# Cross-attention and feed-forward block on one core: adapters accumulated in the base banks, statistics shared between DVE and ACT, written order for PE and DVE, paired transposes

## The chip, the cores and the metric

The kernel runs on one core of one Trainium2 chip. The metric is the device time of one execution in microseconds (us). PE is the matmul engine, DVE the vector engine, ACT the activation engine, POOL the general-purpose engine, SP the engine that issues the loads and stores. The five run side by side and are tied by semaphores; each one runs its own instructions in order.

## The reference

The block takes x of 16 x 64 tokens with 512 features. The first half is a cross-attention with 32 heads of 128 and a bias per head. The second half is a linear layer with a routed low-rank adapter:

```
x = x + xattn(layernorm(x), ctx, mask, bias)         # 32 heads, S = 64
n = layernorm(x)
base   = n @ base_W.T + base_b                       # 512 -> 512
probs  = softmax(n @ router_W.T + router_b)          # 15 routes
w      = sum over the top 8 of probs, mapped by expert_map to 8 experts
h      = n @ A.T                                     # 8 experts x rank 16 = 128
lora   = ((h * w) @ B) * 2
x = x + base + lora
```

All of it is in 32-bit floats. A product is made of three matmuls on halves: each operand is split into a high part (rounded to the matmul's format) and the low rest, and high x high, high x low and low x high are summed.

## The kernel before

Tokens are handled as eight tiles of 128 rows (`NT` = 8). Keys, values and queries are computed in a seven-product scheme over blocks. The heads then run in 16 pairs. For each pair a string `steps` sets what stands after what: `S` is the scores and softmax of two heads, `Q` a step of the queries of the next pair, `O` the output projection of one token tile for the previous pair (`proj_o`, six matmuls of 512 columns, and one DVE add into `acc`), `T` the transpose of one head's probabilities (`transpose_p`, four transposes and one ACT copy). After the string comes `pv_mm`, the product of probabilities and values, with four casts on ACT (`oh`) and four subtracts on DVE (`ol`). PE's order is the written one during attention; the other engines are ordered by a scheduler with priorities, where `tc.high_priority(offset=SOON)` moves an instruction ahead.

The feed-forward stage follows. Its weights lie side by side in `bh` and `bl`, 656 columns each: 128 columns of adapter input A, 15 of the router, one empty column (together `NB` = 144) and then 512 of the base layer. A bank of PSUM holds 512, so each tile takes two groups of matmuls: group A with columns 0 to 255 (L583 to L585 with 128x256; the adapter input, the router and the first 112 base columns), and group B with columns 256 to 655 (the same lines with 128x400). Each group is 12 matmuls. For one tile t the steps are:

- `ffn_norm` (L561): on DVE bn_stats (L88), its aggregate (L89), a small add (L91) and, after POOL's power (L92), a small product (L94); then ACT writes the normalised tile xn (L96).
- `ffn_bias` (L567): POOL adds the base bias to the residual tile, giving xb (L569).
- `ffn_in` (L572): PE transposes xn (L100, four transposes), ACT casts to x2h (L68), DVE subtracts to x2l (L69).
- `ffn_a` (L588): group A; then the routing on DVE, line L592 to L612, with one exponential on ACT (L595), the sum of exponentials (L597), its reciprocal (L599), the scaling of the probabilities (L601), the choice of the top 8 (L603 to L606), the weights by expert (L608, L610) and the weighted adapter input hw (L612). ACT copies the first 112 base columns to o1 (L615).
- `ffn_b` (L618): six matmuls of group B; the transpose of hw (L622); its split into hh (ACT) and hl (DVE); the other six matmuls of B; three adapter matmuls of 512 into a third bank (L634 to L636). For the first six tiles ACT copies B to o1 (L628) and POOL adds xb (L629); for the last two POOL adds 112 columns (L631) and DVE the other 400 (L632). DVE then adds the adapter bank (L637), and SP stores the tile (L638).

The written order of the stage is: six output projections of the last pair, with the norms of tiles 0 to 2 among them; the transposes of tile 0, the seventh projection, the transposes of tile 1, group A of tile 0; then a loop over t in which the norm of t+3, the transposes of t+2, group A of t+1 and `ffn_b` of t follow each other. Only POOL keeps this order strictly (`tc.manual_schedule(engines={nc.gpsimd.engine})`); PE, DVE and ACT are ordered by the scheduler.

Of the kernel before, what the change touches and what calls it, by code (L numbers as in the profile page):

```python
# [25 lines left out]
E = 8  # L26
# [6 lines left out]
OUT_AHEAD = 6  # L33
# [12 lines left out]
def xattn_ffn_kernel(ctx: ExitStack, tc: tile.TileContext, x, ctxT, wq, wk, wv, wo, fside, mask,  # L46
# [58 lines left out]
    with ExitStack() as actx:  # L105
# [208 lines left out]
        with tc.manual_schedule(engines={nc.tensor.engine}):  # L314
# [114 lines left out]
            def pv_mm(i, pt, v):  # L429
                ps = [bank() for _ in range(2)]  # L430
                for u in range(NT):
                    for b in range(2):
                        r = slice(b * S, (b + 1) * S)
                        for d in range(0, P, S):
                            c = slice(i * P + d, i * P + d + S)
                            nc.tensor.matmul(ps[b][d:d + S, u * S:(u + 1) * S], lhsT=v[u // 2][r, u % 2, c],  # L436
                                             rhs=pt[r, u, :], start=True, stop=True)
                res = []
                for b in range(2):
                    hl = [blk("o", f"o{c}", F32R) for c in "hl"]  # L440
                    split(hl[0], hl[1], ps[b])
                    res.append(hl)
                return res
# [60 lines left out]
            for p in range(NP):  # L504
# [5 lines left out]
                steps = "SOOOOOOTOTO" if last else "QSQQOOQOQOOQOQOTOT" if p else "SQQQQQTQQT"  # L510
                pts, t, n = [], 0, 0
                for c in steps:
# [5 lines left out]
                    elif c == "Q":  # L518
                        nxt(1)
                        n += 1  # L520
                        if n == 3:
                            w = load_o(p)
                        if n == 7 and p + 2 < NP:
                            after = Queries(load_pair(p + 2), ORDER)
                        if n == 7 and p + 2 == NP:
                            sar = [blk("raw", "sar", F32, (P, 2, NB)) for _ in range(2)]
                            sbw = [blk("raw", "sbw") for _ in range(KC)]
                            for i in range(2):
                                nc.gpsimd.memset(sar[i][:, :, NAR:NB], 0.0)
                                nc.sync.dma_start(out=sar[i][:, :, 0:NAR], in_=arT[:, 2 * i:2 * i + 2])  # L530
                            for kc in range(KC):
                                nc.sync.dma_start(out=sbw[kc], in_=base_wT[:, kc])
                    elif c == "T":
                        pts.append(transpose_p(ps[len(pts)]))
                    else:
                        proj_o(t, *prev)
                        t += 1
                        if last and t == 2:
                            w = load_o(p)
                qs, nxt = nxt, after  # L540
            prev = ([pv_mm(i, pts[i], v) for i in range(2)], w)
# [6 lines left out]
    slb = blk("g", "slb")  # L548
    nc.sync.dma_start(out=slb, in_=lora_b)
# [8 lines left out]
    lbh = fw.tile([P, D], F32R, name="lbh")  # L558
    lbl = fw.tile([P, D], F32R, name="lbl")
    split(lbh, lbl, slb)  # L560
    def ffn_norm(t):  # L561
        xt = acc[:, t, :]
        xn = fs2.tile([P, D], F32, tag="xn", name="xn2", bufs=3)
        norm(fs2, [xn], [xt])
        return xn
# [6 lines left out]
    def ffn_in(xn):  # L572
# [4 lines left out]
        split(x2h, x2l, ps)  # L577
        return x2h, x2l

    def ffn_mm(o, x2h, x2l, w, kcs=range(KC)):  # L580
        for kc in kcs:
            a = x2h[:, kc * P:(kc + 1) * P]
            nc.tensor.matmul(o, lhsT=a, rhs=bh[:, kc, w], start=kc == 0, stop=False)  # L583
            nc.tensor.matmul(o, lhsT=a, rhs=bl[:, kc, w], start=False, stop=False)
            nc.tensor.matmul(o, lhsT=x2l[:, kc * P:(kc + 1) * P], rhs=bh[:, kc, w],  # L585
                             start=False, stop=kc == KC - 1)

    def ffn_a(x2h, x2l):  # L588
        pa = bank()
        ffn_mm(pa[:, 0:NA], x2h, x2l, slice(0, NA))  # L590
# [4 lines left out]
        nc.scalar.activation(lg, lg, AF.Exp, bias=nm)  # L595
        sme = fs2.tile([P, 1], F32, tag="sme", name="sme2")
        nc.vector.tensor_reduce(sme, lg, AX.X, ALU.add)  # L597
        rc = fs2.tile([P, 1], F32, tag="rc", name="rc2")
        nc.vector.reciprocal(rc, sme)  # L599
        pr = fs2.tile([P, NR], F32, tag="pr", name="pr")  # L600
        nc.vector.tensor_scalar(pr, lg, rc, None, ALU.mult)  # L601
        top = fs2.tile([P, 8], F32, tag="top", name="top")
        nc.vector.max(top, pr)  # L603
        rest = fs2.tile([P, NR], F32, tag="rest", name="rest")
        nc.vector.match_replace(rest, top, pr, 0.0)
        nc.vector.tensor_tensor(pr, pr, rest, ALU.subtract)  # L606
        we = fs2.tile([P, E, NR], F32, tag="we", name="we")
        nc.vector.tensor_tensor(we, oneh, pr.unsqueeze(1).to_broadcast([P, E, NR]), ALU.mult)  # L608
# [3 lines left out]
        nc.vector.tensor_tensor(hw, pa[:, 0:E * R].rearrange("p (e r) -> p e r", e=E),  # L612
                                w8.unsqueeze(2).to_broadcast([P, E, R]), ALU.mult)
        o1 = fs2.tile([P, D], F32, tag="o1", name="o1", bufs=4)
        nc.scalar.copy(o1[:, 0:NA - NB], pa[:, NB:NA])  # L615
        return hw, o1

    def ffn_b(t, xb, x2h, x2l, hw, o1):  # L618
        po = bank()[:, 0:NF - NA]
        ffn_mm(po, x2h, x2l, slice(NA, NF), (0, 1))  # L620
# [4 lines left out]
        split(hh, hl, pt[:, 0:P])  # L625
        ffn_mm(po, x2h, x2l, slice(NA, NF), (2, 3))
        if t < NT - 2:
            nc.scalar.copy(o1[:, NA - NB:D], po)  # L628
            nc.gpsimd.tensor_tensor(o1, o1, xb, ALU.add)  # L629
        else:  # L630
            nc.gpsimd.tensor_tensor(o1[:, 0:NA - NB], o1[:, 0:NA - NB], xb[:, 0:NA - NB], ALU.add)  # L631
            nc.vector.tensor_tensor(o1[:, NA - NB:D], xb[:, NA - NB:D], po, ALU.add)  # L632
        pl = bank()
        nc.tensor.matmul(pl, lhsT=hh, rhs=lbh, start=True, stop=False)  # L634
        nc.tensor.matmul(pl, lhsT=hh, rhs=lbl, start=False, stop=False)
        nc.tensor.matmul(pl, lhsT=hl, rhs=lbh, start=False, stop=True)  # L636
        nc.vector.tensor_tensor(o1, o1, pl, ALU.add)  # L637
        nc.sync.dma_start(out=out[t], in_=o1)  # L638

    def out_proj(a, b):  # L640
        for t in range(a, b):
            proj_o(t, *prev)

    xns, xbs, x2s, hws = [], [], [], []
    with tc.manual_schedule(engines={nc.gpsimd.engine}):
        for t in range(OUT_AHEAD):
            out_proj(t, t + 1)
            if t < 3:
                xns.append(ffn_norm(t))
        xbs.append(ffn_bias(0))  # L650
        x2s.append(ffn_in(xns[0]))
        out_proj(OUT_AHEAD, OUT_AHEAD + 1)
        xbs.append(ffn_bias(1))
        x2s.append(ffn_in(xns[1]))
        hws.append(ffn_a(*x2s[0]))
        for t in range(NT):
            if t + OUT_AHEAD + 1 < NT:
                out_proj(t + OUT_AHEAD + 1, t + OUT_AHEAD + 2)
            if t + 3 < NT:
                xns.append(ffn_norm(t + 3))  # L660
            if t + 2 < NT:
                xbs.append(ffn_bias(t + 2))
                x2s.append(ffn_in(xns[t + 2]))
            if t + 1 < NT:
                hws.append(ffn_a(*x2s[t + 1]))
            ffn_b(t, xbs[t], *x2s[t], *hws[t])
# [42 lines left out]
```

## Time and profile before

| what | value |
|---|---|
| median of three runs | 793.68 us (793.59 to 794.07) |
| profiled execution, time | 795.94 us |
| profiled execution, span of the core | 794.2 us |
| granted PE clock | 1.00 |
| PE busy | 778.5 us of the span |
| DVE busy | 589.1 us |
| ACT busy | 413.0 us |
| POOL busy | 144.0 us |
| feed-forward stage (742 to 794 us) | PE 44.99, DVE 43.06, ACT 18.05, POOL 21.95 us busy |

The span is the time of the core's own instructions; the execution's time has what lies around them too. A busy time of PE has overlaps in it: matmuls are pipelined, and one 512-column matmul of this kernel takes 0.39 us but the next one starts 0.23 us later. So PE's cost is read from start to start.

### The profile page before, as it was taken

The numbers are of one execution on the slowest core, as the hardware profiler recorded it, in microseconds if no ns is written. First come the engines' busy times: TensorE is split into PE (matmuls) and PEld (weight loads), VectorE is DVE, ScalarE is ACT, GpSimd is POOL, SyncE is SP. The second block draws the span as 40 slices with busy tenths as digits, with TensorE's granted clock in tenths as the row PEclk, the third lists the DMA queues.
The fourth block names the chain that finished last, engine by engine and source line by source line (L and its number), as shares of the span: only waits on it lengthen the run. The fifth ranks groups of instructions, "written<-read, shape, count | busy, mean of one in ns | idle before, by whom it ended". The sixth has DMA issues, their size and how long they took to land.

```text
span 794.2 us, 18002 instructions
## 1 busy us (share of the span) xinstructions
PE 778.5 (98%) x6944; PEld 673.7 (85%) x6944; DVE 589.1 (74%) x1056; ACT 413.0 (52%) x1154; POOL 144.0 (18%) x146
## 2 busy tenths in 40 slices
PE   7999999999999999999999999999999999999997
PEld 6988999999999999978888888888888888888786
DVE  6997656555557555678878787878777887878986
ACT  6655444454444444674664566455655466456342
POOL 1011000000006002033311332033202230210352
PEclk9999999999999999999999999999999999999999
DMA  7675545454545543375553364335553455241011
GB/s 269 207 244 200 173 159 186 160 186 160 185 160 171 174 159 133 127 237 170 173 170 90 129 186 161 107 124 171 161 157 97 147 175 171 84 148 56 1 42 66
DMA packets 66374, 120.56 MB, mean 152 GB/s; under 512 B 7536, under 2 KB 8176, under 8 KB 66288
## 3 DMA queue, kind: packets, MB, share of 16 engines
q1 hardware_dynamic: 66288, 119.42, 45.8%
q8 instruction: 54, 0.88, 0.5%
q14 instruction: 32, 0.26, 0.1%
HBM read 83.74 MB, written 35.65 MB: 150 GB/s over the span
## 4 chain that ended last, share of the span: by engine, by line
PE 88%; DVE 7%; ACT 2%; DMA 2%; issue 1%; POOL 0%; SPq 0%; ACTq 0%; DVEq 0%; POOLq 0%
PE ps L222 77%; PE pss L404 4%; PE ps L436 4%; PE pst L423 2%; PE yzv L222 1%; ACT p L412 1%; DMA cT<-in_ctxT 1%; DVE o L637 1%; DVE pr L606 1%; DVE x2l L69 1%; DVE nb L94 1%; DVE gl L69 0%; PE pst L100 0%; DVE we L608 0%; DMA so<-in_wo 0%
## 5 line engine op out<-in xcount | busy, mean ns | idle before, releaser
L68 ACT CAST gh<-s 128x512 fp32r<-128x512 f32 (+1 forms) x128 | 65.6, 514 | 147.3 <-PE ps L222 139.3
L69 DVE TENSOR_TENSOR gl<-s,gh 128x512 fp32r<-128x512 f32 (+1 forms) x128 | 73.3, 572 | 44.5 <-ACT gh L68 44.4
L452 DVE TENSOR_TENSOR acc<-acc,ps 128x512 f32<-128x512 f32 x128 | 86.1, 681 | 21.6 <-PE ps L222 20.7
L412 ACT ACTIVATE p<-p,nm 128x64 f32<-128x64 f32 x256 | 85.5, 336 | 31.6 <-DVE nm L409 31.6
L222 PE MATMUL ps<-wh,oh 128*128 128x512 f32 x256 | 101.4, 397 | 0.0
L222 PE MATMUL ps<-wl,oh 128*128 128x512 f32 x256 | 99.9, 391 | 0.0
L222 PE MATMUL ps<-wh,ol 128*128 128x512 f32 x256 | 99.7, 390 | 0.0
L157 POOL TENSOR_TENSOR s<-rq 128x256 f32<-128x256 f32 x32 | 25.2, 788 | 290.4 <-DMA rq<-in_wq 206.5
L395 POOL TENSOR_TENSOR bm<-bm,maskb 128x512 f32<-128x512 f32 x32 | 50.0, 1582 | 73.1 <-DVE maskb L342 40.8
L69 DVE TENSOR_TENSOR gl<-raw,gh 128x512 fp32r<-128x512 f32 x48 | 34.1, 712 | 31.4 <-ACT gh L68 31.4
L222 PEld LDWEIGHTS ps<-wl,oh 128*128 128x128 f32 x256 | 48.1, 188 | 10.1
L222 PEld LDWEIGHTS ps<-wh,ol 128*128 128x128 f32 x256 | 48.1, 188 | 9.9 <-DVE ol L69 0.5
L222 PEld LDWEIGHTS ps<-wh,oh 128*128 128x128 f32 x256 | 48.1, 188 | 9.5
L68 ACT CAST gh<-raw 128x512 fp32r<-128x512 f32 x48 | 29.7, 621 | 47.8 <-PE ps L222 36.6
L69 DVE TENSOR_TENSOR ol<-ps,oh 128x512 fp32r<-128x512 f32 x64 | 39.8, 683 | 15.6 <-ACT oh L68 15.6
L412 ACT ACTIVATION_READ_ACCUMULATOR p<-p,nm 128x1 f32 x256 | 48.1, 188 | 0.0
L69 DVE TENSOR_TENSOR gl<-rq,gh 128x256 fp32r<-128x256 f32 x48 | 32.9, 687 | 11.4 <-ACT gh L68 11.4
L479 DVE TENSOR_TENSOR q<-u,ps 128x512 f32<-128x512 f32 x48 | 32.6, 680 | 10.6 <-PE ps L222 10.6
L68 ACT CAST oh<-ps 128x512 fp32r<-128x512 f32 x64 | 33.1, 590 | 7.7 <-PE ps L436 7.7
L92 POOL TENSOR_TENSOR rs<-rs,nhalf 128x1 f32<-128x1 f32 x16 | 9.5, 595 | 152.1 <-DVE rs L91 109.2
L404 PEld LDWEIGHTS pss<-kT,q 128*64 128x64 f32 x1024 | 31.2, 138 | 5.6 <-PE ps L222 5.0
L436 PEld LDWEIGHTS ps<-pt,v 64*64 64x64 f32 x2048 | 31.4, 135 | 3.3 <-ACT gh L68 2.2
(226 smaller groups left out, 2273.7 us busy)
## 6 DMA issues: line engine op xcount, KB each, us to landing
kd<-c SPq DMA_DIRECT2D x64, 256.0 KB, 2.6
vd<-c SPq DMA_DIRECT2D x64, 256.0 KB, 2.8
v<-vd SPq DMA_DIRECT2D x64, 256.0 KB, 4.3
kT<-kd SPq DMA_DIRECT2D x64, 256.0 KB, 5.4
raw<-in_wk SPq DMA_DIRECT2D x32, 256.0 KB, 3.0
raw<-in_wv SPq DMA_DIRECT2D x32, 256.0 KB, 3.0
bm<-in_fside SPq DMA_DIRECT2D x32, 256.0 KB, 5.7
rq<-in_wq SPq DMA_DIRECT2D x32, 256.0 KB, 5.5
```

What stands on the lines that cost most here:

```text
L68: nc.scalar.copy(hi, src)
L69: (lo_eng or nc.vector).tensor_tensor(lo, src, hi.bitcast(F32), ALU.subtract)
L92: nc.gpsimd.tensor_tensor(rs, rs, nhalf[:, 0:n], ALU.pow)
L157: self.eng.tensor_tensor(r, a, b, op)
L222: nc.tensor.matmul(o, lhsT=a, rhs=b, start=first and n == 0, stop=last and n == 2, skip_group_check=True)
L395: nc.gpsimd.tensor_tensor(bm, bm, maskb, ALU.add)
L404: nc.tensor.matmul(ps[a * S:(a + 1) * S, t, :], lhsT=qT[n // 8][:, c], rhs=kT[n // 8][:, c], start=True, stop=True)
L412: nc.scalar.activation(p[:, t, :], p[:, t, :], AF.Exp, bias=nm[:, t:t + 1], accum_out=sme[:, t:t + 1])
L423: nc.tensor.transpose(ps[:, g * P:(g + 1) * P], p[:, 2 * g:2 * g + 2, :].rearrange("p t k -> p (t k)"), ident)
L436: nc.tensor.matmul(ps[b][d:d + S, u * S:(u + 1) * S], lhsT=v[u // 2][r, u % 2, c], rhs=pt[r, u, :], start=True, stop=True)
L452: nc.vector.tensor_tensor(acc[:, t, :], acc[:, t, :], ps, ALU.add)
L479: nc.vector.tensor_tensor(self.blocks[key], s[u], b[bk], ALU.add)
```

## The change

Five things are done at once.

1. The adapter's product goes into the two banks that already hold the base layer. The weights `lbh` and `lbl` are widened from 512 to 656 columns with zeros in the first 144, and a tile's three adapter matmuls of 512 into a third bank become three of 400 into B's bank and three of 256 into A's bank. ACT's two copies to o1 and POOL's add go away. DVE adds xb to 400 columns from B's bank and to 112 from A's bank. The last tile's two parts are stored apart, one from SP and one from ACT.
2. The statistics of tiles 0 to 2 stay on DVE, now with priority. Those of tiles 3 to 7 go to ACT: one pass that sums, one that sums the squares of the differences, with small steps on ACT and POOL between them.
3. In the routing, the exponential's own accumulator gives the sum, and the reciprocal is applied in the last product instead of in a step of its own.
4. The order of the feed-forward stage is written: PE and POOL from its start, DVE too from the loop on. Five output projections stand ahead of tile 0's transposes instead of six, and nine matmuls of B stand behind the transpose of hw instead of six. The previous pair's eighth output projection is moved behind the last pair's `pv_mm`, whose results go to another pool. The load of the adapter's weights is issued during the last pair but one.
5. In the 14 middle pairs the two transposes `T` stand next to each other: `...OQOTOT` becomes `...OQOTTO`.

```diff
-            def pv_mm(i, pt, v):
+            def pv_mm(i, pt, v, home="o"):
...
-                steps = "SOOOOOOTOTO" if last else "QSQQOOQOQOOQOQOTOT" if p else "SQQQQQTQQT"
+                steps = "SOOOOOOTOT" if last else "QSQQOOQOQOOQOQOTTO" if p else "SQQQQQTQQT"
...
                             sbw = [blk("raw", "sbw") for _ in range(KC)]
+                            slb = blk("g", "slb")
+                            nc.sync.dma_start(out=slb, in_=lora_b)
...
-            prev = ([pv_mm(i, pts[i], v) for i in range(2)], w)
+            now = ([pv_mm(i, pts[i], v, "g") for i in range(2)], w)
+            proj_o(t, *prev)
+            prev = now
...
-    lbh = fw.tile([P, D], F32R, name="lbh")
-    lbl = fw.tile([P, D], F32R, name="lbl")
-    split(lbh, lbl, slb)
+    lbh = fw.tile([P, NF], F32R, name="lbh")
+    lbl = fw.tile([P, NF], F32R, name="lbl")
+    for half in (lbh, lbl):
+        nc.gpsimd.memset(half[:, 0:NB].bitcast(F32), 0.0)
+    split(lbh[:, NB:NF], lbl[:, NB:NF], slb)
...
     def ffn_norm(t):
...
-        norm(fs2, [xn], [xt])
+        if t < 3:
+            with tc.high_priority(offset=SOON):
+                norm(fs2, [xn], [xt])
+            return xn
+        st = fs2.tile([P, 5], F32, tag="st", name="st", bufs=3)
+        total, nm, sq, rs, nb = (st[:, i:i + 1] for i in range(5))
+        nc.scalar.activation(xn, xt, AF.Identity, accum_out=total)
+        nc.scalar.activation(nm, total, AF.Identity, scale=-1.0 / D)
+        nc.scalar.activation(xn, xt, AF.Square, bias=nm, accum_out=sq)
+        nc.gpsimd.tensor_scalar(rs, sq, 1.0 / D, EPS, ALU.mult, ALU.add)
+        nc.gpsimd.tensor_tensor(rs, rs, nhalf[:, 0:1], ALU.pow)
+        nc.scalar.activation(nb, nm, AF.Identity, scale=rs)
+        nc.scalar.activation(xn, xt, AF.Identity, bias=nb, scale=rs)
         return xn
...
-        nc.scalar.activation(lg, lg, AF.Exp, bias=nm)
         sme = fs2.tile([P, 1], F32, tag="sme", name="sme2")
-        nc.vector.tensor_reduce(sme, lg, AX.X, ALU.add)
+        nc.scalar.activation(lg, lg, AF.Exp, bias=nm, accum_out=sme)
...
-        nc.vector.tensor_scalar(pr, lg, rc, None, ALU.mult)
...
-        nc.vector.tensor_tensor(hw, pa[:, 0:E * R].rearrange("p (e r) -> p e r", e=E),
-                                w8.unsqueeze(2).to_broadcast([P, E, R]), ALU.mult)
-        o1 = fs2.tile([P, D], F32, tag="o1", name="o1", bufs=4)
-        nc.scalar.copy(o1[:, 0:NA - NB], pa[:, NB:NA])
+        nc.vector.scalar_tensor_tensor(hw, pa[:, 0:E * R].rearrange("p (e r) -> p e r", e=E), rc,
+                                       w8.unsqueeze(2).to_broadcast([P, E, R]), ALU.mult, ALU.mult)
...
+    def ffn_lora(o, hh, hl, w):
+        mm(o, hh, lbh[:, w])
+        mm(o, hh, lbl[:, w])
+        mm(o, hl, lbh[:, w], stop=True)
+
+    def ffn_out(t, xb, pa, po):
+        o1 = fs2.tile([P, D], F32, tag="o1", name="o1", bufs=4)
+        for c, src in ((slice(NA - NB, D), po), (slice(0, NA - NB), pa[:, NB:NA])):
+            nc.vector.tensor_tensor(o1[:, c], xb[:, c], src, ALU.add)
+            if t + 1 == NT:
+                (nc.sync if c.start else nc.scalar).dma_start(out=out[t, :, c], in_=o1[:, c])
+        if t + 1 < NT:
+            nc.sync.dma_start(out=out[t], in_=o1)
...
+    with tc.manual_schedule(engines={nc.gpsimd.engine, nc.tensor.engine}):
+        for t in range(5):
+            out_norm(t)
+        turned(0)
+        out_norm(5)
+        turned(1)
+        first(0)
+        hw = ffn_weight(*ffn_route(pas[0]))
+        out_norm(6)
+    with tc.manual_schedule(engines={nc.gpsimd.engine, nc.tensor.engine, nc.vector.engine}):
         for t in range(NT):
+            turned(t + 2)
+            first(t + 1)
+            if t == 0:
+                out_norm(7)
+            if t + 1 < NT:
+                r = ffn_route(pas[t + 1])
+            n = 1 if t else 2
+            po = bank()[:, 0:NF - NA]
+            ffn_mm(po, *x2s[t], B, range(n))
+            hh, hl = ffn_turn(hw)
+            ffn_mm(po, *x2s[t], B, range(n, KC))
+            if t + 1 < NT:
+                hw = ffn_weight(*r)
+            ffn_lora(po, hh, hl, B)
+            ffn_lora(pas[t][:, A], hh, hl, A)
+            ffn_out(t, xbs[t], pas[t], po)
```

Here `out_norm(t)` is `proj_o` and `ffn_norm` of tile t; `turned(t)` is `ffn_bias` and `ffn_in`; `first(t)` is group A; `ffn_turn` is the transpose of hw and its split into hh and hl; `ffn_route` and `ffn_weight` are the two halves of the former routing, up to the exponential and from the reciprocal to hw. The splits of xn's and hw's transposes have priority. One switch of `n` is in it: tile 0 has six matmuls of B ahead of hw's transpose, the others three.

## The prediction

> **What bounds the kernel now.** I read the page first, then busy time by stretches, then the last 52 us with the waits of PE, the chain, and the timelines of PE, DVE, ACT and POOL.
>
> ```profile
> PE 778.5 (98%) x6944; PEld 673.7 (85%) x6944; DVE 589.1 (74%) x1056; ACT 413.0 (52%) x1154; POOL 144.0 (18%) x146
> ```
>
> 98% is an average. By stretches (width, then busy us of PE, weight loads, DVE, ACT, POOL, then granted clock and DMA):
>
> ```profile
> 404.00:690.00 286.00, 285.99 (x3294) 238.62 (x3296) 228.28 (x376) 158.10 (x564) 68.60 (x66) 1.00 0.46 144
> 690.00:742.00 52.00, 51.55 (x617) 42.40 (x608) 42.76 (x79) 27.37 (x97) 3.85 (x6) 1.00 0.30 95
> 742.00:794.00 52.00, 44.99 (x269) 38.43 (x267) 43.06 (x146) 18.05 (x45) 21.95 (x22) 1.00 0.11 41
> ```
>
> The attention pairs are PE without a gap at full clock. Only the feed-forward stage has room. Cut from the start of one tile's first group of matmuls (L583, 128x256) to the next:
>
> ```profile
> 755.45:760.58 5.13, 5.01 (x33) 4.44 (x32) 4.51 (x16) 2.00 (x5) 1.75 (x2) 1.00 0.14 53
> 760.58:766.31 5.73, 5.39 (x36) 4.51 (x34) 5.00 (x19) 2.44 (x6) 3.54 (x4) 1.00 0.12 46
> 771.42:777.09 5.67, 5.37 (x35) 4.50 (x34) 4.99 (x16) 2.49 (x6) 3.67 (x4) 1.00 0.13 49
> 777.09:781.89 4.80, 4.75 (x32) 4.24 (x30) 3.88 (x16) 1.70 (x5) 1.82 (x3) 1.00 0.14 55
> ```
>
> Periods swing between 4.8 and 5.7 us; in the long ones DVE is busy for 5.0. Who makes PE's weight loads wait from 742 to 790.5 (us, times, longest):
>
> ```profile
> PEld ps L636 <- DVE hl L69: 4.5, 7, 1.3
> PEld ps L634 <- ACT hh L68: 1.2, 3, 0.5
> PEld ps L585 <- DVE x2l L69: 1.0, 1, 1.0
> PEld pt L622 <- PE ps L585: 0.8, 1, 0.8
> PEld pt L622 <- DVE hw L612: 0.7, 1, 0.7
> ```
>
> So PE waits for small pieces that stand in DVE's queue. The chain, and POOL beside it, show what holds DVE (start, us):
>
> ```profile
> 759.83 0.16 DVE rest L605
> 759.99 0.02 issue
> 760.01 1.22 DVE pr L606
> ```
> ```profile
> 759.90 1.28 POOL L629 TENSOR_TENSOR o<-o,xb 128x512 f32<-128x512 f32 x1 [3.38 <-ACT o L628]
> 761.14 0.55 POOL L92 TENSOR_TENSOR rs<-rs,nhalf 128x1 f32<-128x1 f32 x1
> 761.66 1.29 POOL L569 TENSOR_TENSOR xb<-acc,bb 128x512 f32<-128x512 f32 x1
> ```
>
> L606 subtracts 15 columns: 0.17 when free, 1.22 while POOL adds two SBUF tiles. DVE adds with a PSUM operand (L637, 762.09) run through POOL's 761.66 add unharmed.
>
> **PE's own work.** Costs from start to start in PE's timeline: four transposes of xn 0.35 (776.74 to 777.09); A (12 matmuls of 256) 1.50 after transposes, 1.42 else; B (12 of 400, 0.181 each) with the transpose of hw 2.29; adapters (three of 512) 0.69; an out-projection O (six of 512) 1.37, after transposes 1.47. From 741.98 (transposes of tile 0) to 790.46 before holds 8x0.35 + 11.9 + 8x2.29 + 8x0.69 + 2.84 = 41.4 us of it in 48.5: 7.1 us are lost.
>
> **The change, part by part.**
>
> *Adapters in the base banks.* Per tile three matmuls of 512 become three of 400 and three of 256: 3x0.181 + 3x0.118 = 0.90, with a switch 0.94 against 0.69. Cost on PE: 8x0.25 = **+2.0**. Gone: ACT's two copies (0.25, 0.50), POOL's add (1.28) and DVE's 0.60 add (spacing); new on DVE are two adds with PSUM, 0.48 as L632 and about 0.2. The two memsets and the wider lbh lie on an idle POOL well ahead.
>
> *Routing.* The sum of exponentials comes from ACT's accumulator (reading it: 0.19 in L412's rows), scaling L601 disappears into the last product: 0.18 + 0.24 off DVE's chain of some 2.9. *Nine matmuls* of B instead of six follow hw's transpose (1.63 against 1.08), to cover hh and hl.
>
> *Written order.* PE goes transposes(t+2), A(t+1), three of B(t), hw(t), nine of B(t), adapters(t). Set A(t+1)'s end at 0: lg and nm of t+1 to 0.4, exp to 0.75; hw(t) turned at 0.54, hh by 1.2, hl by 1.4; PE needs hl at 0.54+0.13+1.63 = 2.3. Then rc, max, replace, subtract, multiply, reduce, product: hw(t+1) at 3.05 to 3.4; PE asks for it at the next A's end + 0.54, over 5 later (for tile 7, whose predecessor has no A behind it, at about 3.8). POOL's next xb waits for the add that frees its slot, and runs while DVE reads PSUM. DVE has 3.7 of work per tile (x2l 0.60, lg and nm 0.4, hl 0.2, rc 0.2, max 0.27, replace 0.26, subtract 0.2, multiply and reduce 0.64, product 0.22, two adds 0.68). Behind hl's wait on DVE stand the whole weighting of the next tile and the output adds; they have 1.4 us of slack. So PE sets the period: 0.35+1.50+0.54+1.76+0.94 = 5.09.
>
> *Statistics of tiles 3 to 7 on ACT.* Off DVE: five of bn_stats 0.60, aggregate 0.09, L91 0.07, L94 (0.07, up to 1.24 behind POOL): at least 4 us. On: per tile two passes, two small ones, and a POOL multiply-add ahead of the power. The nearest rows: xn with two pointers 0.82, reading the accumulator 0.19, L92 0.55. The Trainium skill (ScalarE: Activation LUTs, What ACT_TABLE_LOAD costs) gives 186 ns + 0.833 per element, 93 per pointer; estimated from it, a pass without pointer takes 0.61, with one 0.71, small ones 0.2 to 0.28. Its row for xn would be 0.80 against 0.82 here, so I use them. The same page, Rules for kernel authors, speaks against the move: adds and multiplies belong on VectorE. By it, 5x(0.70+0.22+0.80+0.28) = 10 us on ACT replace 4 us on DVE. By the rows, ACT works 18 us of 52, DVE 43 and PE waits for DVE: the move pays unless a PE input stands behind it. One does.
>
> ACT's order, with times by layout from 737.9: xn of 0 to 2; x2h(0) 740.9; sums of 3, x2h(1), squares of 3 to 743.6, sums of 4; POOL's two operations (pow 0.55; the multiply-add unknown, between 0.1 and 0.55, I take 0.25 as nearest to a small op; with two hand-overs 1.0); nb(3) 744.65; exp(0) 745.0; xn(3); squares of 4 to 746.85; x2h(2); nb(4) waits for POOL to 747.85; sums of 5, xn(4), squares of 5 to 750.45; nb(5) waits to 751.45; exp(1); **hh(0) 751.9 to 752.15**. PE finishes B(0) at 750.55 and needs hh(0): **a stall of 1.6 us**, once. Nothing on PE can pass it. Behind ACT's wait for nb(5) stand exp(1), hh(0), xn(5) and x2h(3), and POOL's first bias add now stands behind two tiles' powers (needed only at 753). hw(0) is out at 748.0 and asked for at 749.3. For tiles 1 and 2 hh comes before nb's wait, about 2.5 after xn's transposes; needed at 4.0. Bounds of the stall: 0 (POOL and ACT faster) to 3.5 (0.6 more on each of three trips).
>
> *The tail of attention.* O7 of the previous pair now stands behind the last PV product and covers the cast of o: PE lost 0.5 there (733.30 to 735.83 for nine matmuls). PE also lost 0.26 on pt behind ACT's wh (715.74), and 0.16 at 729.33; adjacent transposes put both pt ahead of wh, and the freed DVE order brings nm(0) earlier: 0.4 together. Tile 0's xn is ready at 738.8, before its transposes at 739.63: O5 moves behind them, and x2l(0), which made PE wait 0.8, costs 0.1. Cover gone, these 0.8 come back. slb's load is issued some 16 us earlier on SP, ahead of an sbw load, bb and the two so loads; SP waits 6.9 us for a buffer before so, so nothing is later.
>
> *Two transposes together*, 14 pairs. From 686.136 T, O, T up to PV took 0.35 + 1.48 + 0.53 = 2.36. T, T, O up to PV by the same rows: 0.43 (transposes stand 0.108 apart) + 0.35 + 1.48 + 0.08 (from O to PV at 730.96 it is 0.31 for 0.23) = 2.34. p of the second head is ready at 676.7, its transpose at 688.0: no wait. I take -0.1 in all; bounds are one switch of 0.09 a pair either way, 1.3. ACT's pt passes two gh casts, 0.5 later, needed 2 later.
>
> *The end.* Last, DVE adds 400 and then 112 columns, 0.45 after PE's end instead of 0.77, and two transfers go out on SP and ACT. Their rows are 1600 and 448 bytes. The trace has 2.0 us for 2 KB rows; the skill (DMA: Bandwidth & Descriptors, first table) asks for 512 bytes to avoid read-modify-write. By the row -0.3; by the rule a few tenths of that are lost on 57 KB. I take -0.3, bound 0.
>
> **The sum.** PE from transposes(0) at 739.63: 41.4 + one more O 1.37 + 2.0 = 44.8, stalls 0.1 + 1.6, gives 786.1 against 790.46: -4.3. End -0.3, pairs -0.1: **-4.7**. The profiled execution took 795.94 (span 794.2); that becomes 791.2. The median of the runs, 793.68, lies 2.3 below the profiled one; the same difference gives **789.0**.
>
> **Rivals.**
> 1. *No stall at hh(0), and the pairs gain their bound*: POOL's trips hide. -4.7 - 1.6 = -6.3, with 1.2 more on the pairs -7.5: 786.2 to 787.4. For: ACT idles 65% of the stage. Against: three in-order waits in 12 us. 0.22.
> 2. *The written order brings small waits every tile*: hl(1) comes 0.2 before its need at tile 1, xb(1) and xb(2) block the subtract; 0.3 a tile returns 2.4: 791.4. With a stall of 3.5 instead of 1.6, 790.9. 0.17.
> 3. *Nothing to measure*: both kinds of wait together, 3.1 to 6.3 in sum, eat the gain: 792.1 to 795.3. 0.07. That adapters or statistics don't run as written is excluded by the listed instructions; a second table load for the squares is not among them either.
> 4. *Slower: ACT is the bound.* A statistics tile costs ACT 4.1 (0.70+0.22+0.80+0.28+0.82+0.59+0.41+0.25) plus POOL's 1.0: 5.1, as much as PE's period. Each further us of POOL's trip goes through all five. From a trip of about 1.9 the five take the 4.7 back; at 2.5 it is 5x1.5 = 7.5 less 4.7, so 796.5. Against: L92's median is 0.55, its longest 0.88. 0.06.
>
> **Numbers.** The layout itself 0.48, between 788.2 and 790. About 0.2% (1.6 us) is what a measurement of this kernel tells from none. Faster 0.87, same 0.07, slower 0.06. The range for 8 in 10 runs from 786.2 (rival 1) to 792.0 (past rival 2, to where a gain can still be told).
>
> **Right or wrong.** In the new profile: periods of PE near 5.1 from tile 1 to 5; one wait of the 400-column adapters for hh L67 near 1.6; no POOL add on o; DVE under 80% in the stage; transposes(0) about 2.3 earlier. Periods over 5.5, or ACT's nb waiting for POOL over 2 us, would show the forecast wrong.

## The result, and the profile after

The kernel after takes 789.53 us (median of 6 runs, 789.09 to 790.50) where the kernel before took 793.59 beside it: a ratio of 0.9952, 95% interval 0.9939 to 0.9964. That is 4.1 us off, against a forecast of 4.7; the forecast time was 789.0.

The profiled execution of the kernel after has a span of 787.6 us and took 789.44. Its span is 6.5 shorter than the profiled one of before, but 2.5 of that lie ahead of the first pair of heads (its scores start at 335.54 instead of 338.00), in code that is the same. The scores of pair 1 start anywhere from 353.7 to 356.8 in the profiled executions of this case, and at 354.8 and 356.8 in two of one and the same kernel (e10_split_stats and e10_again). Even the stretch from pair 0 to pair 1 takes 17.4 to 20.2. So I measure from landmarks in PE's timeline from there on: the scores of pair 1, those of pair 14 and of the last pair, the first transpose of tile 0, the end of PE's last matmul, the end of the span.

| from, to | before | after | difference | forecast |
|---|---|---|---|---|
| pair 1 to pair 14 | 335.82 | 335.78 | 0.0 | -0.1 |
| pair 14 to the last pair | 24.72 | 24.22 | -0.5 | -0.3 |
| last pair to PE's end | 73.62 | 70.64 | -3.0 | -4.0 |
| PE's end to the end of the span | 3.70 | 3.25 | -0.45 | -0.3 |
| sum | | | -4.0 | -4.7 |

Of the 0.4 that the prediction gave to the tail of attention, the 0.26 for pt (715.74 before) lies between pair 14 and the last pair; the rest is counted behind it.

The page's first line, which stood at PE 778.5, DVE 589.1, ACT 413.0 and POOL 144.0 before:

```profile
PE 776.4 (99%) x6968; PEld 675.6 (86%) x6968; DVE 576.9 (73%) x1026; ACT 417.2 (53%) x1178; POOL 138.9 (18%) x145
```

PE issues 24 matmuls more (three more in each of eight tiles) and DVE is 12 us lighter. Busy time by stretches, cut at the transposes of tile 0 (columns as before: width, busy us and count of PE, weight loads, DVE, ACT, POOL, then granted clock and DMA):

```profile
689.00:737.04 48.04, 48.04 (x565) 39.86 (x564) 39.55 (x75) 25.77 (x93) 4.67 (x8) 1.00 0.32 99
737.04:787.60 50.56, 45.84 (x299) 43.27 (x297) 32.87 (x120) 23.17 (x69) 14.35 (x19) 1.00 0.12 43
```

In the feed-forward stage DVE works 32.9 us of 50.6, where it worked 43.1 of 52.0; ACT has gained 5, POOL has lost 7.6. The same stage by periods of PE, from one first group of 256 columns to the next:

```profile
751.23:756.28 5.05, 5.05 (x39) 5.01 (x37) 4.47 (x19) 3.89 (x11) 1.02 (x3) 1.00 0.14 52
756.28:761.33 5.05, 5.05 (x38) 5.01 (x37) 3.90 (x13) 3.79 (x11) 2.31 (x4) 1.00 0.14 52
761.33:766.64 5.31, 5.31 (x39) 4.91 (x37) 4.45 (x16) 1.14 (x4) 2.23 (x2) 1.00 0.14 51
766.64:771.69 5.05, 5.05 (x38) 5.01 (x37) 4.19 (x17) 1.14 (x4) 1.29 (x1) 1.00 0.15 55
```

The swing between 4.8 and 5.7 is gone: 5.05, and once 5.31. PE's busy time fills all four windows; the 0.25 of the third lies in a late start that the modelled ends of the matmuls cover. What PE still waits for from 700 us on, matmuls first, then weight loads (us, times, longest):

```profile
PE ps L599 <- ACT hh L67: 1.2, 1, 1.2
PE ps L599 <- DVE x2l L68: 0.2, 1, 0.2
```
```profile
PEld ps L599 <- ACT hh L67: 1.8, 2, 1.5
PEld ps L599 <- DVE x2l L68: 0.4, 1, 0.4
PEld ps L599 <- ACT x2h L67: 0.4, 1, 0.4
```

DVE's hl, 4.5 us in seven waits before, is no longer in the list. One wait of 1.2 for hh stands in its place, the one that the forecast put at 1.6. ACT's timeline shows its cause (start, length, idle time ahead and who ended it):

```profile
747.94 0.19 ACT L577 ACTIVATION_READ_ACCUMULATOR xn<-acc,st 128x1 f32 x1
749.07 0.29 ACT L580 ACTIVATE st<-st 128x1 f32<-128x1 f32 x1 [0.94 <-POOL st L579]
749.27 0.29 ACT L614 ACTIVATE lg<-lg,nm 128x15 f32<-128x15 f32 x1
749.47 0.19 ACT L614 ACTIVATION_READ_ACCUMULATOR lg<-lg,nm 128x1 f32 x1
749.56 0.24 ACT L67 CAST hh<-pt 128x128 fp32r<-128x128 f32 x1
```

The transposed hw was there at 747.6. hh is cast at 749.56, because ACT's queue holds tile 5's statistics ahead of it, and their step at L580 (nb) waits 0.94 for POOL. The next tile's exponential (L614) stands in front too.

The period of 5.31 was not forecast. POOL and DVE, around 760:

```profile
759.73 2.53 POOL L586 TENSOR_TENSOR xb<-acc,bb 128x512 f32<-128x512 f32 x2
```
```profile
759.88 1.17 DVE L624 TENSOR_TENSOR lg<-lg,rest 128x15 f32<-128x15 f32 x1
761.08 1.32 DVE L626 TENSOR_TENSOR we<-oneh,lg 128x120 f32<-128x120 f32 x1
```

POOL's written order puts tile 7's powers ahead of two bias additions, which then run back to back. Two small DVE steps with both inputs in SBUF, 0.17 and 0.28 when free, last 1.17 and 1.32. Everything behind them on DVE comes 2 us later. ACT has the next tile's exponential ahead of hh and waits for DVE with it until 764.68, so hh of tile 3 just misses its moment: 0.25 us, once.

### The profile page after: what moved, and what is told of

Its sections match the earlier page's. It is cut to its first block, busy times and chain, and to the rows that moved or that the text cites. A ratio compares the mean times of both kernels' runs of the same rounds, so it can differ in the third digit from the quotient of the medians.

```text
span 787.6 us, 18020 instructions
## 1 busy us (share of the span) xinstructions
PE 776.4 (99%) x6968; PEld 675.6 (86%) x6968; DVE 576.9 (73%) x1026; ACT 417.2 (53%) x1178; POOL 138.9 (18%) x145
## 4 chain that ended last, share of the span: by engine, by line
PE 92%; DVE 3%; ACT 3%; DMA 1%; issue 1%; POOL 1%; DVEq 0%; POOLq 0%; ACTq 0%
PE ps L221 77%; PE ps L435 4%; PE pss L403 4%; PE ps L599 4%; PE pst L422 2%; DVE gl L68 1%; PE yzv L221 1%; ACT p L411 1%; PE pst L99 0%; DMA raw<-in_wk 0%; DMA vd<-c 0%; ACT xn L577 0%; POOL rs L91 0%; PE pt L99 0%; DMA kd<-c 0%
## 5 line engine op out<-in xcount | busy, mean ns | idle before, releaser
L394 POOL TENSOR_TENSOR bm<-bm,maskb 128x512 f32<-128x512 f32 x32 | 52.0, 1644 | 71.4 <-DVE maskb L341 39.5
L68 DVE TENSOR_TENSOR gl<-rq,gh 128x256 fp32r<-128x256 f32 x48 | 31.3, 654 | 17.8 <-ACT gh L67 17.8
L68 DVE TENSOR_TENSOR wl<-so,wh 128x512 fp32r<-128x512 f32 x32 | 36.0, 1126 | 0.0
```

The lines of the kernel that those rows point to most:

```text
L68: (lo_eng or nc.vector).tensor_tensor(lo, src, hi.bitcast(F32), ALU.subtract)
L394: nc.gpsimd.tensor_tensor(bm, bm, maskb, ALU.add)
```

## The experiments

All ratios are to the kernel before, run beside each of them. The later runs were made where the kernel before took 794.1 to 794.7, so their times are not set against 789.5; the ratios and the stretches between landmarks are. "Tail" is the stretch from the last pair's scores to PE's end: 73.62 before, 70.64 after.

| kernel | tail, us | PE's end to end of span | ratio, 95% interval |
|---|---|---|---|
| after | 70.64 | 3.25 | 0.9952 (0.9939 to 0.9964) |
| after_again | 70.64 | 3.24 | 0.996 (0.9946 to 0.9974) |
| e1_apart | 70.62 | 3.25 | 0.9964 (0.995 to 0.9978) |
| e5_order_only | 77.44 | 3.68 | 1.0037 (1.0023 to 1.0051) |
| e8_fold_only | 73.19 | 3.39 | 0.9978 (0.997 to 0.9986) |
| e3_stats_dve | 72.81 | 3.25 | 0.998 (0.997 to 0.9991) |
| e4_third_bank | 71.81 | 3.87 | 0.9965 (0.9954 to 0.9976) |
| e6_late_stats | 71.37 | 3.26 | 0.9943 (0.9923 to 0.9962) |
| e7_late_third | 71.54 | 3.85 | 0.9957 (0.994 to 0.9973) |
| e9_late_dve | 69.88 | 3.24 | 0.9926 (0.9908 to 0.9944) |
| e10_split_stats | 69.07 | 3.24 | 0.994 (0.9925 to 0.9956) |
| e10_again | 69.07 | 3.25 | 0.9939 (0.992 to 0.9958) |
| e11_mixed_bank | 69.17 | 3.24 | 0.9946 (0.9932 to 0.9961) |

The tails repeat within 0.02 us (after twice, and e1_apart; e10 twice), while whole executions of one kernel spread over 1.4 to 5.7 us. So a mechanism is judged by the tail and its waits, and the ratio says whether it reaches the whole. Every other tail comes from one profiled execution.

> The kernel after once more, unchanged, beside the two that follow. Its ratio should fall in the interval measured first, 0.9939 to 0.9964; the stretch from the last pair's scores to PE's end should again be 70.6, with one wait of 1.2 for hh.

As expected. The first interval and this one overlap.

### e1_apart: the pairs' transposes

```diff
-                steps = "SOOOOOOTOT" if last else "QSQQOOQOQOOQOQOTTO" if p else "SQQQQQTQQT"
+                steps = "SOOOOOOTOT" if last else "QSQQOOQOQOOQOQOTOT" if p else "SQQQQQTQQT"
```

> The kernel after, with the two transposes of the middle pairs set apart again as before; the last pair and the feed-forward are as after. Theory (the pairs gained nothing but their hand-over to the last pair): all pairs stay at 25.81 us, at most the interval from pair 14 to pair 15 goes from 24.22 back towards 24.7; total 789.5 to 790.1, that is 0 to 0.5 above the kernel after. Rival (keeping the transposes together spared a switch of about 0.08 us in each of 15 pairs): pairs 25.85 to 25.9 and a total of 790.7 or more.

The theory holds. Pairs take 25.81 in both, the tail is 70.62, and also the interval before the last pair stays at 24.22. So the adjacent transposes gain nothing at all, and the 0.5 us of that interval does not come from them either. It comes from ACT's order: before, the cast of wh, which had waited for its load, stood ahead of the copy to pt that PE needs; in the kernel after and here pt stands ahead. ACT before, then in e1_apart:

```profile
714.58 0.62 ACT L68 CAST wh<-so 128x512 fp32r<-128x512 f32 x1 [0.89 <-DMA so<-in_wo]
715.10 0.58 ACT L426 COPY pt<-pst 128x512 f32<-128x512 f32 x1
```
```profile
714.34 0.59 ACT L425 COPY pt<-pst 128x512 f32<-128x512 f32 x1 [0.26 <-PE pst L422]
714.82 1.14 ACT L67 CAST wh<-so 128x512 fp32r<-128x512 f32 x2
```

PE's wait of 0.26 for pt at 715.74 is gone with it. In e8_fold_only, where wh is still cast first, the interval is 24.54. Which part of the new order moved pt ahead was not tried alone.

### e5_order_only and e8_fold_only: each half alone

e5_order_only has the order of the kernel after with the tile's work of the kernel before (statistics on DVE, third bank, copies, additions on POOL, and the old routing, whose lines are left out here):

```diff
-        if t < 3:
+        if t < NT:
...
-            ffn_lora(po, hh, hl, B)
-            ffn_lora(pas[t][:, A], hh, hl, A)
+            pl = bank()
+            mm(pl, hh, lbh, True)
+            mm(pl, hh, lbl)
+            mm(pl, hl, lbh, stop=True)
...
+        nc.scalar.copy(o1[:, 0:NA - NB], pa[:, NB:NA])
+        if t < NT - 2:
+            nc.scalar.copy(o1[:, NA - NB:D], po)
+            nc.gpsimd.tensor_tensor(o1, o1, xb, ALU.add)
...
+        nc.vector.tensor_tensor(o1, o1, pl, ALU.add)
```

> The order of the kernel after (its written order, the last pair's o-projection moved, the transposes together) with the work of the kernel before: all statistics on DVE, adapters in a third bank, copies on ACT and additions of o on POOL. Theory (the lighter DVE carries the gain): the feed-forward keeps most of its waits of hl, hh and x2l, total 791.5 to 793. Rival (the order carries it): waits are gone with the old work too, total 789.0 to 790.5.

Both missed: it is slower than the kernel before, by 0.37% (2.9 us of 794). PE waits 3.82 us for the first hw, and later 0.6 to 0.8 for those of tiles 5 to 7. In DVE's queue the priority statistics of tiles 5 to 7 had been put in among the first routing.

e8_fold_only leaves the kernel before as it is, order and statistics too, and only folds the adapters and adds o on DVE:

```diff
-        pl = bank()
-        nc.tensor.matmul(pl, lhsT=hh, rhs=lbh, start=True, stop=False)
...
+        ffn_lora(po, hh, hl, B)
+        ffn_lora(pa[:, A], hh, hl, A)
+        for c, src in ((slice(NA - NB, D), po), (slice(0, NA - NB), pa[:, NB:NA])):
+            nc.vector.tensor_tensor(o1[:, c], xb[:, c], src, ALU.add)
```

> The kernel before with only the adapters folded into the base banks and o added on DVE from the two banks (no copies on ACT, no third bank, no addition of o on POOL); its statistics, its order and its pairs as before. Theory (relief of DVE from POOL's additions carries most): the feed-forward's waits of 6.9 us fall to 3 or less against 2.0 more work on PE, total 1.5 to 2.5 below the kernel before. Rival (statistics and order carry it): the waits stay above 5 and the total is 0 to 2 above the kernel before.

The total falls as the theory says (0.22%, 1.7 us; 0.9 between the landmarks), but not for its reason. PE's waits for hl all but end:

```profile
PEld ps L566 <- ACT hh L68: 2.4, 4, 0.8
PEld ps L566 <- DVE x2l L69: 1.0, 1, 1.0
PEld ps L566 <- DVE hl L69: 0.8, 2, 0.4
```

hl is down from 4.5 to 0.8, hh is up from 1.2 to 2.4. By start spacings PE lost about 7 us in the tail before and still loses about 5 here, not 3 or less. That gain of about 2 is little more than what the fold costs PE (1.6, from e4_third_bank below).

So the order alone gives +2.9 us and the fold alone -1.7, which makes +1.2. The two together, with the new routing, are e3_stats_dve below: 1.6 under the kernel before. So the parts don't add up, unless the routing alone brings the missing 2.8; no run has it alone. ACT's statistics, on top of that, make it -4.1.

### e3_stats_dve: ACT's share taken back

```diff
-        if t < 3:
+        if t < NT:
```

> The kernel after, with the statistics of all eight tiles on DVE and none on ACT and POOL. Theory A (DVE would be full again with them, ACT's five tiles are what made room): the feed-forward's period grows and the total is 1.5 to 3 above the kernel after, about 791.5. Theory B (DVE has room once the copies and the third-bank additions are gone, and the share of ACT only brings its wait of 1.2 us for the first tile's hh): that wait goes, the periods stay at 5.05, total about 788.5, 1.0 below the kernel after.

Theory A's total came (0.998 against 0.9952; the tail is 2.2 us longer), but by luck: the periods don't grow. They stay at 5.03 to 5.05 and the hh wait did go, as theory B says, so DVE is not too full. DVE's timeline shows where the time went:

```profile
742.43 1.23 DVE L93 SCALAR_TENSOR_TENSOR nb<-mv,rs 128x1 f32<-128x1 f32 x1
...
745.40 1.24 DVE L93 SCALAR_TENSOR_TENSOR nb<-mv,rs 128x1 f32<-128x1 f32 x1 [0.66 <-POOL rs L91]
746.57 0.67 DVE L451 TENSOR_TENSOR acc<-acc,ps 128x512 f32<-128x512 f32 x1
747.16 0.15 DVE L619 RECIPROCAL rc<-sme 128x1 f32<-128x1 f32 x1
...
748.32 0.69 DVE L68 TENSOR_TENSOR x2l<-pt,x2h 128x512 fp32r<-128x512 f32 x1
...
749.82 0.35 DVE L630 SCALAR_TENSOR_TENSOR hw<-ps,rc,w 128x128 f32<-128x128 f32 x1
```

Here, ahead of the loop, DVE is still ordered by priorities. Tile 5's last statistics step waits 0.66 for POOL and then runs 1.24 beside POOL's addition of xb; the first routing, whose exponential was ready at 745.0, begins behind it, and x2l of tile 2 is put in between. hw is asked for at 747.9 and read at 750.32. And the wait costs more than its length. PE's first matmul behind it, then PE alone in slices of 2 us (busy, then granted clock, DMA share, GB/s):

```profile
750.32 0.30 PE L636 MATMUL pt<-ident,hw 128*128 128x128 f32 x1 [2.26 <-DVE hw L630]
```
```profile
748.00:750.00 2.00, 0.06 (x1) 1.00 0.00 0
750.00:752.00 2.00, 1.68 (x7) 0.69 0.00 0
752.00:754.00 2.00, 1.77 (x6) 0.50 0.00 0
754.00:756.00 2.00, 2.00 (x19) 0.96 0.00 0
```

After 2.26 us without work PE is granted about half its clock for a while: the slices add up to 1.7 us of clock lost, which is 3.4 us at half. A matmul of 400 columns then starts every 0.33 us instead of 0.18. From the turning of hw to the next transposes it is 4.0 us here and 3.55 after; without their waits (0.4, and 1.3 for hh) 3.6 against 2.2, so the clock took 1.4 of the 2.2 us. In e5_order_only the wait of 3.82 is followed by 0.63, 0.50, 0.50 and 0.66 in four such slices, 3.4 us lost. And e1_apart has the same in code that all these kernels share, just ahead of the scores of pair 1, after a wait of 2.00:

```profile
347.44 0.50 PE L221 MATMUL ps<-t4h,gh 128*128 128x512 f32 x1 [2.00 <-ACT u L471]
```
```profile
347.00:349.00 2.00, 1.56 (x5) 0.83 0.36 130
349.00:351.00 2.00, 2.00 (x6) 0.50 0.35 119
351.00:353.00 2.00, 2.00 (x46) 0.82 0.42 120
```

The longest waits of PE in these traces that leave every slice at 1.00 are 1.68 (here, at 348.9) and 1.64 (e6_late_stats). So the limit lies between 1.7 and 2.0 us, as far as three long waits can tell. The Trainium skill (TensorE: Matmul & The Clock Gate, Why this matters for your kernels) sets it at gaps of about 3 us, which is too long here.

The 22 executions of e3_stats_dve don't all pay alike. The six with a mean clock of 0.996 or less have a median of 794.7 us, the four with 1.000 one of 792.1; the profiled one has 0.998. So 1.4 is what the clock took in this one execution.

### e4_third_bank: what the fold costs on PE

```diff
-            ffn_lora(po, hh, hl, B)
-            ffn_lora(pas[t][:, A], hh, hl, A)
-            ffn_out(t, xbs[t], pas[t], po)
+            pl = bank()
+            mm(pl, hh, lbh, True)
+            mm(pl, hh, lbl)
+            mm(pl, hl, lbh, stop=True)
+            ffn_out(t, xbs[t], pas[t], po, pl)
...
+        nc.vector.tensor_tensor(o1, o1, pl, ALU.add)
```

> The kernel after, with the adapters in a third bank of PSUM again (three banks of 512 columns, one LDWEIGHTS and MATMUL less per tile) and one more addition on DVE for each tile; statistics shared as after. Theory (the folded adapters cost PE 0.25 us a tile, and DVE now has room for the addition): period 5.05 goes to 4.8, total 1.5 to 2.0 below the kernel after, about 787.7. Rival (the added 0.7 us on DVE makes hl and x2l late again): DVE waits of 0.3 to 0.5 a tile come back and the total is 0 to 1 above the kernel after.

(The edit takes three matmuls a tile away, not one.) Periods are 4.86 to 4.89 where nothing waits, so the fold costs PE 0.2 us a tile, not 0.25: 1.6 in all. But the loss that the rival expects comes too, for hh and hw rather than for hl and x2l:

```profile
PE ps L597 <- ACT hh L67: 2.2, 3, 1.1
PE pt L634 <- DVE hw L628: 0.4, 1, 0.4
```

The added 0.69 on DVE makes the next routing late, and ACT's in-order queue had that routing's exponential ahead of hh. At 761.08 one DVE step is held behind POOL (1.32), and with the addition on top hh of tile 3 comes 0.93 too late: a period of 6.07. The end is 0.6 later as well (3.87), with one addition more behind PE. Tail +1.2, instead of -1.6.

### e6_late_stats and e7_late_third: ACT's order written out

```diff
-        xns[t] = ffn_norm(t)
+        if t < 5:
+            xns[t] = ffn_norm(t)
...
-    with tc.manual_schedule(engines={nc.gpsimd.engine, nc.tensor.engine, nc.vector.engine}):
+    with tc.manual_schedule(engines={nc.gpsimd.engine, nc.tensor.engine, nc.vector.engine, nc.scalar.engine}):
...
-            if t + 1 < NT:
-                r = ffn_route(pas[t + 1])
...
             hh, hl = ffn_turn(hw)
+            if t + 1 < NT:
+                r = ffn_route(pas[t + 1])
+            if t < 3:
+                xns[t + 5] = ffn_norm(t + 5)
```

> The kernel after, where ACT's order in the feed-forward is written out too: the statistics of tiles 5 to 7 come on ACT behind the first three tiles' hh, and a tile's hh and hl stand ahead of the next tile's routing. Theory (the first hh waited 1.2 us only because ACT's queue had a statistics step in front of it that waited for POOL, and the later 0.15 came from a routing in front of an hh): both waits go, the stretch from the last pair's scores to PE's end is 1.3 to 1.5 shorter than the 70.64 of the kernel after, about 69.2, ratio to the kernel before 0.9935. Rival (the statistics, now in front of the next x2h on ACT, hold x2h and behind it DVE's hl): a new wait of 0.5 or more for hl or hw, 69.9 to 71.

The first hh has no wait left, so the cause of the 1.2 us is shown. But the sum is the rival's and a little more: weight loads wait 1.3 for hl and 1.0 for hh, the periods of tiles 1 to 3 are 5.37, 5.89 and 5.90, the tail is 71.37, 0.7 longer than after. ACT:

```profile
758.81 0.19 ACT L577 ACTIVATION_READ_ACCUMULATOR xn<-acc,st 128x1 f32 x1
759.94 0.29 ACT L580 ACTIVATE st<-st 128x1 f32<-128x1 f32 x1 [0.94 <-POOL st L579]
760.26 0.81 ACT L581 ACTIVATE xn<-acc,st 128x512 f32<-128x512 f32 x1
760.99 0.56 ACT L67 CAST x2h<-pt 128x512 fp32r<-128x512 f32 x1
761.45 0.27 ACT L67 CAST hh<-pt 128x128 fp32r<-128x128 f32 x1
```

The same 0.94 for POOL now stands, with the pass behind it, in front of x2h and hh. ACT's statistics of a tile are a chain of five steps with a trip to POOL in it, and in both places where they were put in ACT's queue something waits behind. Splitting this chain around the trip was not tried. The ratio, 0.9943, does not show the 0.7; its interval covers both.

> The order of e6_late_stats with the adapters in a third bank and a third addition on DVE for each tile. Theory (in e4_third_bank the third bank saved PE 0.19 to 0.25 us a tile and lost it to hh behind a late routing on ACT): with hh ahead of the routing the periods are 4.85 and no hh waits are left; the stretch from the last pair's scores to PE's end is about 67.7, and 0.6 comes back at the store, so 1.0 less than e6_late_stats in all. Rival (DVE itself is too full with the third addition): waits for hl, x2l or hw of 0.2 or more a tile, and no gain over e6_late_stats.

The rival holds: no gain over e6_late_stats. Periods are 4.86 once the statistics are over, but hh waits of 0.5 remain in tiles 2 and 3 behind ACT's statistics, and the last hw is late by 0.9.

### e9_late_dve and e10_split_stats: all statistics on DVE, in the right place

e9_late_dve is e6_late_stats with `if t < NT` instead of `if t < 3` in the statistics.

> The order of e6_late_stats with all statistics on DVE, those of tiles 5 to 7 behind the next tile's routing. Theory (DVE has room for them; in e3_stats_dve only their place in front of the first routing cost): no wait over 0.5 for hw, total within 0.5 of e6_late_stats. Rival (DVE needs ACT's share): hw is late in tiles 1 to 3 or the first hw again waits 1 or more, total 1.5 or more above e6_late_stats.

No wait over 0.3 for hw, and it beats e6_late_stats, whose order it shares, by 1.5 us in the tail, where the theory expected no more than 0.5 either way; the kernel after it beats by 0.8. DVE has the room; e3_stats_dve lost by place. Tiles 1 to 3 take 5.28 to 5.38, and DVE's timeline shows why:

```profile
754.43 0.16 DVE L90 TENSOR_SCALAR rs<-mv 128x1 f32<-128x1 f32 x1
755.32 0.16 DVE L93 SCALAR_TENSOR_TENSOR nb<-mv,rs 128x1 f32<-128x1 f32 x1 [0.73 <-POOL rs L91]
755.39 0.16 DVE L619 RECIPROCAL rc<-sme 128x1 f32<-128x1 f32 x1
```

DVE stands 0.73 for POOL's power with the routing ready behind it. e10_split_stats moves that one step behind the routing's product: `norm_begin` goes up to POOL's power, `norm_end` holds nb and xn.

```diff
             if t < 3:
-                xns[t + 5] = ffn_norm(t + 5)
+                late = norm_begin(acc[:, t + 5, :])
...
                 hw = ffn_weight(*r)
+            if t < 3:
+                xns[t + 5] = norm_end(acc[:, t + 5, :], *late)
```

> As e9_late_dve, but DVE's last step of the late statistics (the one that waits for POOL) stands behind the weights of the next tile, so that DVE does not stand idle for POOL. Theory (in tiles 1 to 3 DVE was full, 5.28 us a tile with 0.73 of waiting for POOL): those periods fall from 5.28 to 5.05, the waits for hw of 0.2 go, the stretch from the last pair's scores to PE's end is 69.2 to 69.3. Rival (the wait moves with the step and holds the additions of o, x2l and hl instead): 69.8 or more.

The theory holds, but for one tile (5.22): periods 5.04, 5.02, 5.22, 5.06 (e9_late_dve: 5.38, 5.28, 5.29, 5.04), and all that PE waits for from 700 us on is

```profile
PE ps L616 <- DVE x2l L68: 0.3, 1, 0.3
PE pt L653 <- DVE hw L647: 0.2, 1, 0.2
```

Tail 69.07, 1.57 under the kernel after.

> e10_split_stats once more, unchanged, to see whether its lead over the kernel after shows in whole executions too. Theory (the 1.57 us between the landmarks of the two traces are real): ratio to the kernel before 0.9925 to 0.9945. Rival (spread of whole executions hides it or it was chance): 0.995 to 0.997.

The same tail and ratio (0.9939). Between landmarks e10_split_stats beats both kernels. In whole executions its two ratios, 0.994 and 0.9939, lie under the two of the kernel after, 0.9952 and 0.996, by some 0.15% (1.3 us), but the intervals overlap: likely, not settled. Its 0.8 against e9_late_dve (0.9926) does not show in whole executions at all.

### e11_mixed_bank

```diff
-            ffn_lora(po, hh, hl, B)
-            ffn_lora(pas[t][:, A], hh, hl, A)
+            if 3 <= t < 6:
+                pl = bank()
+                mm(pl, hh, lbh[:, NB:NF], True)
+                mm(pl, hh, lbl[:, NB:NF])
+                mm(pl, hl, lbh[:, NB:NF], stop=True)
+            else:
+                ffn_lora(po, hh, hl, B)
+                ffn_lora(pas[t][:, A], hh, hl, A)
...
+        if pl is not None:
+            nc.vector.tensor_tensor(o1, o1, pl, ALU.add)
```

> As e10_split_stats, with the adapters in a third bank for tiles 3 to 5 alone, where DVE has no statistics and no end of the kernel behind it. Theory (a third bank spares PE 0.2 us a tile wherever DVE has room for one more addition of 0.69): three periods go from 5.05 to 4.85, 0.6 less than e10_split_stats in all. Rival (the additions make the last tiles' hw late, as in e7_late_third, where the last waited 1.1): 0 to 1 more than e10_split_stats.

The rival: periods of 4.91 and 4.85 come as hoped, and the last two tiles wait for hw (0.7 us longest) and give them back. At the end PE's period shrinks to 3.2 to 4.6, since no further tile's work lies between, and DVE's chain to hw sets the pace.

## Why the prediction was right

**Where the time was and why it came.** PE waited for small pieces in DVE's queue; the lighter queue in a written order removes those waits. That holds in the wait lists, hl from 4.5 us to none, and in the sum: from the transposes of tile 0 on PE loses 2.9 us where it lost 7.1, against 1.7 more work. The signs named in advance came too: periods of 5.05, one wait for hh, no POOL addition on o, DVE busy for 65% of the stage, the transposes of tile 0 2.4 earlier counted from pair 14. But the parts don't each work alone, as the sum, which prices them one by one, suggests: the order with DVE's old work is slower than before.

**The fold, +2.0 on PE.** Measured 1.6 to 1.7: periods of 4.86 without it and 5.05 with it, and a tile's six adapter matmuls take 0.90 from start to start instead of the 0.94 assumed. The period itself, forecast at 5.09, is 5.05.

**The stall at hh(0), 1.6.** Right in cause and place; PE stood idle 1.16, and the next start came 1.32 later than normal. It is smaller because PE asked later, not because hh came sooner. Counted from the first transposes, hh was ready after 12.8 us (12.5 forecast), but PE, which had lost more than forecast at tile 0, needed it after 11.5 (10.9 forecast). POOL's trip took 0.94 (1.0 assumed), its multiply-add 0.19 (0.25). The ACT passes estimated at 0.61 and 0.71 took 0.63 and 0.72, the small ones 0.20 and 0.29.

**x2l(0), 0.1.** This step failed: the first group of tile 0 loses 0.9 by start spacings (0.38 waiting for x2h, 0.39 for x2l, and 0.1 because the matmul behind a wait was followed after 0.22 instead of 0.12). The prediction had x2h(0) ready 1.3 after the start of the transposes; it was ready after 2.5, because ACT had tile 2's xn in front of it while the transposes were out at 737.6:

```profile
738.27 0.82 ACT L95 ACTIVATE xn<-acc,nb,rs 128x512 f32<-128x512 f32 x1 [0.36 <-DVE nb L93]
739.00 0.56 ACT L67 CAST x2h<-pt 128x512 fp32r<-128x512 f32 x1
```

In e9_late_dve and e10_split_stats x2h no longer waits there.

**The period of tile 3.** The prediction let xb run while DVE reads PSUM; once two of them ran together over SBUF-only steps instead. 0.25. It was named in rival 2 for xb(1) and xb(2) and priced there, not in the sum.

**The sum for the stage.** From the transposes of tile 0 to PE's end 46.5 was forecast and 47.36 measured: +0.8 at tile 0, -0.2 at hh, +0.25 at tile 3, -0.3 for the fold, +0.15 because the last matmul ends 0.28 after its start, and 0.2 spread over the other rows. (The prediction's own terms give -4.4 for the stage and -4.8 in all; it wrote -4.3 and -4.7.) This 0.9 and the missing 0.1 of the pairs, less the better end (-0.45 for -0.3), are what lies between the forecast and the measured -4.0.

**Pairs -0.1, tail of attention, end -0.3.** The pairs gained nothing. From pair 14 to the transposes of tile 0 the kernel gains 1.0 us besides the output projection that moved behind them, as forecast (0.9 to 1.0): pt ahead of wh holds, and was worth 0.5 instead of 0.26, but the reason given for it (adjacent transposes) is refuted by e1_apart. The end measured -0.45. The stores of 1600-byte and 448-byte rows landed after 1.9 us each, against 2.0 for full rows, so the rule on 512 bytes that the prediction weighed (the Trainium skill, DMA: Bandwidth & Descriptors, first table) took nothing that could be seen.

**The argument for ACT.** "The move pays unless a PE input stands behind it" was right, and the exception was larger than the rule. Against statistics left on DVE with priority (e3_stats_dve) ACT's share is worth 2.2 us. In one and the same order (e6_late_stats against e9_late_dve) it costs 1.5, and the kernel after, which has it, is 0.8 to 1.6 behind e9_late_dve and e10_split_stats. So the rule that the prediction weighed and set aside (the Trainium skill, ScalarE: Activation LUTs, Rules for kernel authors: adds and multiplies belong on VectorE) was the better guide here, once the order was free to be chosen. The page gives the speed per element as its reason; here it was what stood behind the steps in ACT's queue.

**Rivals.** The first (no stall) did not come, nor the gain of the pairs; the second came in part (one tile, 0.25); the third (nothing to measure) did not, the interval ends at 0.9964; the fourth did not: POOL's trip stayed at 0.94, under the 1.9 from which it decides.

## What to carry to other kernels

When work is moved to an idle engine, ask not how busy that engine is but what stands behind the moved step in its queue, above all if the step waits for a third engine: a wait of 0.9 us held hh and x2h in turn, in both places where ACT's five steps were put. On DVE the same statistics stopped costing once the one step that waits was split off and placed behind the piece that PE needs. Measure parts both alone and together before crediting one. And a wait of PE isn't priced by its length alone: look at the granted clock in the slices behind it.

## What the hardware showed that was not expected

- An idle PE of 2.00 or 2.26 us is followed by 3.4 us at half the granted clock (1.7 us of clock lost), one of 3.82 by twice that; up to 1.68 us it brings nothing. So a stall can cost more than its length, in e3_stats_dve by 1.4 us.
- Two POOL additions in a row (2.53 us) held two DVE steps in a row, 0.17 and 0.28 when free, for 1.17 and 1.32. Both have two SBUF inputs.
- Code that is the same in all kernels reached the scores of pair 1 between 353.7 and 356.8 us: a difference of 3.1 us before the changed part begins, as large as most effects studied here. In e1_apart, at 356.0, a wait of 2.00 and the slower clock behind it are part of that.
